# Tracing the stages of an edge step from the oldest quad to the newest

## The chip, the cores and the metric

The kernel runs on one core of a Trainium2 chip. Its time is the device time of one execution in microseconds; a kernel's time is the median of its runs. Before the change it is 5046.02 us (11 runs, 5038.25 to 5059.39). The engines are TensorE (PE in the profile, its weight loads PEld), VectorE (DVE), ScalarE (ACT), GpSimd (POOL) and the DMA queue of SyncE (SP). Each takes its instructions in a fixed order, and an instruction that waits holds those behind it on its engine.

## The reference

Two graph layers over 12,500 nodes of 64 features and 400,000 edges sorted by `dst`. The first is an edge-conditioned message layer with a residual and layer norms, the second two rounds of degree-normalized neighbour sums, a linear layer and another norm:

```python
x_t = _mlp2(x, W1n, b1n, W2n, b2n)
e_t = _mlp2(edge_attr, W1e, b1e, W2e, b2e)      # 32 -> 64 -> 64, leaky_relu 0.1
msgs = x_t[src] * e_t * dp_scale
aggregated = jax.ops.segment_sum(msgs, dst, num_segments=num_nodes)
out = x + aggregated * res_w                    # then layer norm, gamma, beta
...
x = _layernorm(x + out)
...
for _ in range(2):
    msgs = edge_weight[:, None] * h[col]
    h = jax.ops.segment_sum(msgs, row, num_segments=n)
x = _layernorm(x + (h @ W.T + b))
```

`edge_weight` is the product of the inverse square roots of the degrees of the two ends; every node also has a loop to itself.

## The kernel before

**Three phases.** First comes a short one with the node network, whose output goes to a table in DRAM, `xt_tab`. The edge phase follows, to about 4262 us, then the second hop, to the end (5049 us), which is matmuls on TensorE (lines 1221 and 1232) over the adjacency that the edge phase has written to DRAM.

**The edge phase** goes through the edges in "quads" of 12 chunks of 128 edges, 261 quads from the last edge to the first. A quad passes four stages:

- `hidden` (first layer of the edge network): two products on PE into two PSUM banks `pw` (line 624), ACT scales them into `z` (634), DVE takes the maximum (638). `z` has two buffers, the edge features `eat` have three; their load (line 614, SP's queue) is issued two steps ahead and needs the buffer of the quad three before to be free.
- `message`, in two halves: the second layer on PE into a bank `pe` (bias 648, product 650), then DVE multiplies it by the gathered node rows `xg` into `msgs` (659). `xg` has four buffers.
- `level1`: DVE compares the destinations with a range of 32 (one-hot, 674), PE sums the messages per destination into `pl` (684), ACT copies it to `tot` (693).
- `level2`: a second one-hot (DVE, 703) and matmuls that add `tot` into `ring` (713), an accumulator in one PSUM bank.

One step `t` of the loop traces the stages of four different quads: `hidden` of `order[t]`, `message` of the one before, `level1` of the one two before and `level2` of the one three before. Around these five units (two of them are the halves of `message`) it interleaves other work. The step is cut into 15 slots, three to a unit; a unit is traced at the first of its three slots. Each of the first 12 slots traces one gather (line 592): an indirect DMA on POOL of 128 rows of `xt_tab` for the quad two steps ahead. Then the slot traces its share of two generators. `adjacency` builds the dense adjacency by one-hot matmuls (DVE 859 and 910, PE 920, ACT 935, store 944), and `hop1` multiplies finished parts of it (PE 1117, 1129, 1246). After the units come, when the adjacency is done, up to three `scatter_store` preparations for the second hop (DVE 1055, 1059 and 1069, PE 1062 and 1078, ACT 1081), and every ten steps or so the norm of finished nodes (`nodes`, from line 757 on), which reads and clears part of `ring`.

**What sets the order.** The program is traced in this order, and a planner then puts each engine's instructions into their final order by a simulated timeline; units are traced with a priority 500 ahead of the rest. All PSUM users but `ring` share seven banks under one tag.

**The pace of the gathers** is set by hand. `marks` lists the last matmul of each finished message half and of each finished adjacency block, in traced order; when a gather is traced, the one eight before it is made to wait for the mark traced last:

```python
gates.append(got)
if len(gates) > GATE and marks:          # GATE = 8
    tc.add_manual_dep(gates[-GATE - 1], marks[-1].name, ...)
```

`a_target` spreads the adjacency so that it is done about ten steps before the last quad (`LEAD`); after that only messages put down marks.

Of the kernel before, what the change touches and what calls it, by code (L numbers as in the profile page):

```python
# [35 lines left out]
NQ = -(-NCH // QC)  # L36
# [162 lines left out]
def tile_fast(  # L199
# [327 lines left out]
    def bank(shape, name):  # L527

        n = math.prod(shape[1:])
        t = banks.tile([P, 512], F32, name=name, tag="bank")[:, :n]  # L530
        if len(shape) == 3:
            t = t.rearrange("p (a b) -> p a b", b=shape[2])
        elif len(shape) == 4:
            t = t.rearrange("p (a b c) -> p a b c", b=shape[2], c=shape[3])
        return t
# [81 lines left out]
    def hidden(q):  # L617
        def f():
            z = hs[q] = edgep.tile([P, 2, SCC * P], F32, name="z")
            ea_q = eas.pop(q)  # L620
            pws = [bank([P, SCC * P], f"pw{h}") for h in range(2)]
            for h in range(2):
                rows = slice(D * h, D * (h + 1))
                nc.tensor.matmul(  # L624
                    pws[h],
                    w1ab[rows, h, :],
                    ea_q[rows],
                    start=True,
                    stop=True,
                    tile_position=(D * h, 0),  # L630
                )

            for h in range(2):
                nc.scalar.activation(  # L634
                    z[:, h, :], pws[h], AF.Identity, bias=b1s, scale=SLOPE
                )
            for h in range(2):
                nc.vector.scalar_tensor_tensor(  # L638
                    z[:, h, :], pws[h], b1, z[:, h, :], op0=ALU.add, op1=ALU.max
                )  # L640

        return f

    def message(q, h):
        def f():
            z = hs[q]
            pe = bank([P, 2, SCC, D], "pe")
            nc.tensor.matmul(pe, ones_b, b2p, start=True, stop=False)
            for c in range(SCC):
                ended = nc.tensor.matmul(  # L650
                    pe[:, :, c, :],
                    z[:, h, c * P : (c + 1) * P],
                    w2,
                    start=False,
                    stop=(c == SCC - 1),
                )
            marks.append(ended.ins)
            k = 2 * SCC
            nc.vector.tensor_mul(  # L659
                msgs[q % 3][:, k * h : k * (h + 1), :D],  # L660
                pe.rearrange("p s c d -> p (s c) d"),
                xgs[q][:, k * h : k * (h + 1), :],
            )
            if h == 1:
                del hs[q], xgs[q]

        return f

    def level1(q):
        def f():  # L670
            _, rel = seg[q // SEGQ]
            c0 = (q % SEGQ) * QC
            oh = edgep.tile([P, QC, REL], F32, name="oh1")
            nc.vector.tensor_tensor(
                oh,
                iota_f[:, None, :REL].to_broadcast([P, QC, REL]),
                rel[:, c0 : c0 + QC, None].to_broadcast([P, QC, REL]),
                op=ALU.is_equal,
            )
            pl = bank([P, D + 1], "pl")  # L680
            m = msgs[q % 3]
            for s in range(4):
                for c in range(SCC):
                    nc.tensor.matmul(  # L684
                        pl[REL * s : REL * (s + 1), :],
                        oh[:, s * SCC + c, :],
                        m[:, s * SCC + c, :],
                        start=(c == 0),
                        stop=(c == SCC - 1),
                        tile_position=(0, REL * s),  # L690
                    )
            tot = edgep.tile([P, D + 1], F32, name="tot")
            nc.scalar.copy(tot, pl)
            tots[q] = tot

        return f

    def level2(q):
        def f():
            lo, hi = QWIN[q]  # L700
            n = hi - lo + 1
            oh = edgep.tile([P, 4 * P], F32, name="oh2")
            nc.vector.tensor_scalar(
                oh[:, : n * P],
                iota_f[:, : n * P],
                float(P * lo),
                qn[:, q : q + 1],
                op0=ALU.add,
                op1=ALU.is_equal,
            )  # L710
            tot = tots.pop(q)
            for w in range(lo, hi + 1):
                nc.tensor.matmul(
                    ring[:, w % RING, :],
                    oh[:, (w - lo) * P : (w - lo + 1) * P],
                    tot,
                    start=False,
                    stop=False,
                    skip_group_check=True,
                )  # L720

        return f
# [562 lines left out]
    order = list(range(NQ - 1, -1, -1))  # L1285
# [8 lines left out]
    def take(q):  # L1294

        k = q // SEGQ
        if k not in seg:
            load_seg(k)
        load_ea(q)
        return gathers(q)  # L1300
# [30 lines left out]
    for t in range(NQ + 3):  # L1331
        units = []
        if t + PRE < NQ:
            more = take(order[t + PRE])
        else:
            more = iter(())
        if t < NQ:
            units += [hidden(order[t])]
        if 0 <= t - 1 < NQ:
            units += [message(order[t - 1], 0), message(order[t - 1], 1)]  # L1340
        if 0 <= t - 2 < NQ:
            units += [level1(order[t - 2])]
        if 0 <= t - 3 < NQ:
            units += [level2(order[t - 3])]
        if 0 <= t - ZERO < 2 * HT:
            with tc.issue_after(last_load[0]):
                zero_table(t - ZERO)
        lead = 1 + (LEAD - 1) * min(1.0, t / RAMP)
        a_target = a_total * min(1.0, (t + lead) / NQ)
        a_step = max(0.0, a_target - a_spent) / max(1, len(units))  # L1350
        h_step = H_RATE / max(1, len(units))
        a_goal, h_budget = a_spent, 0.0
        parts = -(-QC // len(units))
        a_step, h_step = a_step / parts, h_step / parts
        for u in range(parts * len(units)):
            if u % parts == 0:
                with tc.high_priority(PRIO):
                    units[u // parts]()
            next(more, None)
            a_goal += a_step  # L1360
            while a_live and a_spent < a_goal:
                c = next(a_gen, None)
                if c is None:
                    a_live = False
                else:
                    a_spent += c
            h_budget += h_step
            while h_live and h_budget > 0:
                try:
                    c = next(h_gen)  # L1370
                except StopIteration:
                    h_live = False
                    break
                if c is None:
                    h_budget = 0.0
                    break
                h_budget -= c
        for _ in more:
            pass
        if a_spent >= a_total:  # L1380
            if not spc:
                counts.close()
                scatter_start(
                    main.enter_context(tc.tile_pool(name="spp", bufs=1)), bank
                )
                narrow()
                dpools[0] = ctx.enter_context(tc.tile_pool(name="h2e", bufs=H2E, side="right"))
                early = [load_dense(*d, 0) for d in dense[:H2E]]
            for _ in range(PREPS):
                if prepped < EARLY:  # L1390
                    scatter_store(sparse[prepped])
                    prepped += 1

        q_done = order[t - 3] if t >= 3 else None
        if q_done is not None:
            top = QWIN[q_done - 1][1] if q_done > 0 else -1
            while groups and groups[0][0] > top:
                lo, hi = groups.pop(0)
                with tc.high_priority(PRIO if hi <= 5 else 0):
                    nodes(lo, hi)  # L1400
                ln_done[0] = lo
# [950 lines left out]
```

## Time and profile before

| what | us |
|---|---|
| median of 11 runs | 5046.02 |
| the profiled execution | 5050.39 |
| its span in the profile | 5048.7 |
| first gather starts | 70.2 |
| last gather ends on POOL | 4262.0 |
| second hop's matmuls start | 4322.0 |

Shares of the span: PE 87%, POOL 75%, DVE 65%, ACT 45%; mean granted clock of TensorE 0.911. The second part of the page cuts the span into 40 slices of 126 us; each digit is a busy share in tenths, and the PEclk row is the granted clock in tenths:

```profile
PE   5776889989989898988997999697788978999997
DVE  7887778766658686887777787766777756100004
ACT  3887777545545454654554443333322123100003
POOL 6777767777777777777777777777777765688885
PEclk7888999999999898978997999798898967999998
```

The slices 1 to 34 are the node network and the edge phase, the rest the seam and the second hop. A row read across shows which engine is full where; that an engine is below 9 does not show that it waits, since a gather of 0.94 us with its fixed 0.30 us to the next reads as 7.

### The profile page before, as it was taken

Reading aid. Unit: us, or ns where it says so; the run is one execution under the profiler, and the core shown is the slowest. Engines: PE = TensorE matmul, PEld = TensorE weight load, DVE = VectorE, ACT = ScalarE, POOL = GpSimd, SP = SyncE. Lnnn points to the kernel's source line nnn. Section 1 sums busy time; section 2 is a strip of 40 time slices with the busy share of each in tenths; the row PEclk is TensorE's granted clock in tenths of the full one; section 3 lists DMA queues with packets and bytes.
Section 4 is the critical chain, followed back from the end, with each engine's and each line's share of the span. In section 5 each row is a group of like instructions: output and inputs, shape, how many; then the busy total and the mean of one; then the engine's idle time right before and its main releaser. Section 6 shows DMA issues by size and latency. Waiting matters only on the chain. (4 is left out here: it accounts for less than half of the span.)

```text
span 5048.7 us, 94126 instructions
## 1 busy us (share of the span) xinstructions
PE 4410.5 (87%) x31344; PEld 2581.9 (51%) x31344; DVE 3269.0 (65%) x11086; ACT 2265.0 (45%) x7868; POOL 3793.4 (75%) x3607
## 2 busy tenths in 40 slices
PE   5776889989989898988997999697788978999997
PEld 3443455555546465645554555354455555444443
DVE  7887778766658686887777787766777756100004
ACT  3887777545545454654554443333322123100003
POOL 6777767777777777777777777777777765688885
PEclk7888999999999898978997999798898967999998
DMA  5877788766657576646664554353333253999998
GB/s 140 187 166 135 143 160 158 150 129 147 144 127 152 121 152 130 125 85 150 144 126 103 121 127 101 83 120 88 64 79 75 65 145 99 229 211 213 206 200 222
DMA packets 1254835, 696.95 MB, mean 138 GB/s; under 512 B 593468, under 2 KB 1188144, under 8 KB 1253312
## 3 DMA queue, kind: packets, MB, share of 16 engines
q1 hardware_dynamic: 1104032, 566.91, 46.7%
q0 software_dynamic: 150304, 123.92, 16.1%
q8 instruction: 248, 4.06, 0.3%
q14 instruction: 251, 2.06, 0.2%
HBM read 494.67 MB, written 195.83 MB: 137 GB/s over the span
## 5 line engine op out<-in xcount | busy, mean ns | idle before, releaser
L592 POOL DMA_INDIRECT xg<-xt_tab,si x3125 | 3127.3, 1001 | 1006.1 <-issue 467.2
L935 ACT ACTIVATE stage<-pa 128x391 fp8e4<-128x391 f32 x3077 | 1511.7, 540 | 1132.5 <-PE pa L920 1078.8
L910 DVE TENSOR_SCALAR oh<-iota_b,colT 128x391 bf16<-128x391 bf16 x5556 | 1605.1, 333 | 202.9 <-PE pa L920 199.2
L920 PE MATMUL pa<-oh,koh 128*128 128x391 bf16 (+2 forms) x6054 | 1272.8, 368 | 248.5 <-DVE oh L910 72.5
L920 PEld LDWEIGHTS <-koh 128*128 128x128 bf16 (+2 forms) x6054 | 604.1, 150 | 621.7 <-issue 346.4
L935 ACT ACTIVATION_READ_ACCUMULATOR stage<-pa 128x1 f32 x3077 | 746.8, 247 | 0.0
L1117 PE MATMUL hacc_p<-at,gp 128*128 128x512 fp8e4 (+1 forms) x2425 | 642.8, 393 | 89.2 <-ACT gp L744 45.6
L659 DVE TENSOR_TENSOR msg<-pe,xg 128x384 f32<-128x384 f32 x522 | 289.6, 555 | 545.9 <-DMA xg<-xt_tab,si 342.6
L1492 POOL DMA_INDIRECT hop_tab<-tot,first x317 | 493.4, 1556 | 100.6 <-issue 94.2
L650 PEld LDWEIGHTS pe<-w,z 128*128 128x128 f32 x3132 | 461.4, 208 | 74.7 <-issue 52.0
L650 PE MATMUL pe<-w,z 128*128 128x128 f32 x3132 | 472.9, 291 | 0.0
L1221 PE MATMUL acc<-at,gp 128*128 128x512 fp8e4 (+1 forms) x2000 | 445.9, 376 | 0.0
L1117 PEld LDWEIGHTS <-gp 128*128 128x128 bf16 x2425 | 230.8, 102 | 389.4 <-issue 136.0
L859 DVE TENSOR_TENSOR koh<-iota_k,keyT 128x512 bf16<-128x512 bf16 (+3 forms) x920 | 384.2, 419 | 0.0
L634 ACT ACTIVATE z<-pw,b1s 128x384 f32<-128x384 f32 x522 | 292.2, 616 | 204.2 <-PE pw L624 199.7
L684 PE MATMUL pl<-msg,oh 128*32 128x65 f32 x6264 | 281.0, 229 | 111.9 <-DVE msg L659 108.1
L624 PE MATMUL pw<-eat,w1ab 64*128 64x384 f32 x1044 | 362.7, 600 | 12.1 <-DVE msg L659 7.1
L1129 PE MATMUL hacc_p<-at,gp 128*64 128x512 fp8e4 (+1 forms) x2425 | 365.1, 389 | 0.0
L1600 DVE TENSOR_TENSOR pot<-po,dis 128x256 f32<-128x256 f32 (+2 forms) x26 | 10.5, 408 | 538.4 <-PE po L1594 538.4
L638 DVE SCALAR_TENSOR_TENSOR z<-pw,b,z 128x384 f32<-128x384 f32 x522 | 312.5, 607 | 45.6 <-ACT z L634 45.6
L684 PEld LDWEIGHTS pl<-msg,oh 128*32 128x32 f32 x6264 | 228.5, 112 | 210.1 <-DVE msg L659 95.3
L1221 PEld LDWEIGHTS <-gp 128*128 128x128 bf16 x2000 | 188.3, 99 | 227.3 <-issue 28.8
(218 smaller groups left out, 3954.8 us busy)
## 6 DMA issues: line engine op xcount, KB each, us to landing
adj<-stage SPq DMA_DIRECT2D x390, 391.0 KB
at<-adj SPq DMA_DIRECT2D x97, 896.0 KB
at<-adj SPq DMA_DIRECT2D x168, 512.0 KB
eat<-in_eaq_dram SPq DMA_DIRECT2D x261, 192.0 KB
xg<-xt_tab,si POOLq DMA_INDIRECT x3125
at<-adj SPq DMA_DIRECT2D x96, 256.0 KB
at<-adj SPq DMA_DIRECT2D x24, 832.0 KB
at<-adj SPq DMA_DIRECT2D x24, 768.0 KB
```

What stands on the lines that cost most here:

```text
L592: got = nc.gpsimd.indirect_dma_start(out=xg[:, i, :], out_offset=None, in_=xt_tab, in_offset=bass.IndirectOffsetOnAxis(ap=si[:, c : c + 1] ...
L624: nc.tensor.matmul(pws[h], w1ab[rows, h, :], ea_q[rows], start=True, stop=True, tile_position=(D * h, 0),)
L650: ended = nc.tensor.matmul(pe[:, :, c, :], z[:, h, c * P : (c + 1) * P], w2, start=False, stop=(c == SCC - 1),)
L684: nc.tensor.matmul(pl[REL * s : REL * (s + 1), :], oh[:, s * SCC + c, :], m[:, s * SCC + c, :], start=(c == 0), stop=(c == SCC - 1), tile_ ...
L859: nc.vector.tensor_tensor(t[:, :, :n], iota_8[:, :, :n] if w == 8 else iota_k[:, : w * FA, :n], keyT[:, None, j0 : j0 + n].to_broadcast([P ...
L910: nc.vector.tensor_scalar(oh, iota_b, colT[:, i % P : i % P + 1], None, op0=ALU.is_equal)
L920: ended = nc.tensor.matmul(to, key, oh, start=(j == 0), stop=(j == caps[g] - 1), tile_position=(0, r0),)
L935: nc.scalar.activation(stage[:, u, :], pa, AF.Identity, saturate=True, accum_out=sums[:, u : u + 1],)
L1117: nc.tensor.matmul(acc[:, :w], gp[:kk, lo + i, 0:2, :].rearrange("p t d -> p (t d)"), t[:kk, i, :w], start=start, stop=False, skip_group_c ...
L1129: nc.tensor.matmul(acc[D * h : D * (h + 1), :w], gp[:kk, lo + i, 2, :], t[:kk, i, :w], start=False, stop=False, skip_group_check=True, til ...
L1221: nc.tensor.matmul(acc[:, :w], gp[:kk, wi, 0:2, :].rearrange("p t d -> p (t d)"), t[:kk, wi - lo, :w], start=first and n == 0, stop=False, ...
L1492: nc.gpsimd.indirect_dma_start(out=hop_tab[(q * QC + i) % HT], out_offset=bass.IndirectOffsetOnAxis(ap=first[:, q - Q0, i : i + 1], axis=0 ...
```

## The change

Only the order in which a step traces its five units is turned round: level 2 of the oldest of the four quads first, then level 1, the two message halves, and the newest quad's first layer last. Which quads a step works on is as before, as are the gathers, the two generators between the units, the gate and the work after the units.

```diff
@@ -1334,14 +1334,14 @@
             more = take(order[t + PRE])
         else:
             more = iter(())
+        if 0 <= t - 3 < NQ:
+            units += [level2(order[t - 3])]
+        if 0 <= t - 2 < NQ:
+            units += [level1(order[t - 2])]
+        if 0 <= t - 1 < NQ:
+            units += [message(order[t - 1], 0), message(order[t - 1], 1)]
         if t < NQ:
             units += [hidden(order[t])]
-        if 0 <= t - 1 < NQ:
-            units += [message(order[t - 1], 0), message(order[t - 1], 1)]
-        if 0 <= t - 2 < NQ:
-            units += [level1(order[t - 2])]
-        if 0 <= t - 3 < NQ:
-            units += [level2(order[t - 3])]
         if 0 <= t - ZERO < 2 * HT:
             with tc.issue_after(last_load[0]):
                 zero_table(t - ZERO)
```

## The prediction

> **What bounds the kernel now.** I read the page's engine shares first, then its costliest groups, then POOL's waits stretch by stretch, then the busy time by stretch, and last the chain of work around the end of the edge phase. The first lines are from the page and from the view of one source line (L592, the gather of 128 node rows); the columns are busy time, mean ns | idle before, releaser, and below them min/median/max ns.
>
> ```profile
> PE 4410.5 (87%) x31344; PEld 2581.9 (51%) x31344; DVE 3269.0 (65%) x11086; ACT 2265.0 (45%) x7868; POOL 3793.4 (75%) x3607
> L592 POOL DMA_INDIRECT xg<-xt_tab,si x3125 | 3127.3, 1001 | 1006.1 <-issue 467.2
> L592 POOL DMA_INDIRECT xg<-xt_tab,si x3125: 938/944/3579, 70.2 to 4261.1; - x196
> ```
>
> PE has the largest share, but POOL issues gathers one behind the other from 70 us to 4262 us: 3127 busy + 1006 idle = 4133 of 4192 us. Most of that idle time is a fixed 0.30 us ahead of each gather (3125 x 0.30 = 938). So a gather costs 1.30 us and a quad of twelve 15.6 us, and only about 1006 - 938 = 68 us are real waiting. Where it is shows in POOL's waits (total, times, longest) in 500 to 820, 820 to 4040 and 4040 to 4265 us:
>
> ```profile
> POOL xg L592 <- PE pa L920: 41.0, 76, 6.8
> ...
> POOL xg L592 <- PE pa L920: 142.9, 469, 0.3
> ...
> POOL xg L592 <- PE pe L650: 33.8, 9, 9.5
> ```
>
> In the 3200 us in the middle no gather waited beyond its 0.3 us. Beyond 0.3 us each, the early stretch holds 41.0 - 76 x 0.3 = 18.2 us (waiting for adjacency blocks), the late one 33.8 - 9 x 0.3 = 31.1 us (waiting for the messages' matmuls). Busy time by stretch (PE, PEld, DVE, ACT, POOL, granted clock, DMA share, GB/s):
>
> ```profile
> 820.00:2000.00 1180.00, 1103.94 (x8103) 651.27 (x8101) 840.86 (x2856) 630.25 (x2251) 902.06 (x913) 0.95 0.66 140
> 2000.00:4040.00 2040.00, 1760.34 (x12431) 1078.27 (x12429) 1536.44 (x5394) 864.29 (x2868) 1563.31 (x1565) 0.90 0.48 104
> 4040.00:4262.00 222.00, 185.15 (x1257) 127.97 (x1255) 123.21 (x246) 65.86 (x121) 148.28 (x141) 0.66 0.45 126
> 4322.00:5049.00 727.00, 698.16 (x5128) 334.21 (x5126) 79.39 (x148) 75.24 (x202) 568.82 (x380) 0.98 0.92 210
> ```
>
> PE is 94% busy up to 2000 us, 86% up to 4040, and the second hop after 4322 is PE's alone. The chain of waits at the seam:
>
> ```profile
> 4261.10 3.18 DMA xg<-xt_tab,si
> ...
> 4264.40 0.57 DVE msg L659
> ...
> 4310.81 4.82 DMA gw_tab<-gwp
> ...
> 4322.02 3.56 PE acc L1221 x16
> ```
>
> The last gather lands, the last message is multiplied, and 58 us later the second hop starts. So the time is: end of the gathers (4262.0) + tail (60.0) + second hop (726.7) = 5048.7 us, and 1.7 us around the span make the profiled 5050.4. This execution lies 4.4 us above the median of the runs, 5046.0; I make the sum against 5050.4 and subtract 4.4.
>
> **The change part by part.** No instruction is added or removed. Per quad the moved stages issue: hidden 4 PE passes (two fp32 products), 2 ACT, 2 DVE; the two messages 14 PE passes and 2 DVE; level 1 24 PE passes, 1 DVE, 1 ACT; level 2 some 4 PE passes and 1 DVE. None issues a DMA. A step has 15 slots, with adjacency blocks and first-hop batches between the stages. Hidden moves from slot 0 to 12, the messages from 3 and 6 to 6 and 9, level 1 from 9 to 3, level 2 from 12 to 0. The planner may re-sort, but PE holds nearly to the traced order: in one step (time, duration)
>
> ```profile
> 2002.49 0.33 PE L648 MATMUL pe<-b2p,ones_b 128*128 128x384 bf16 x1
> ...
> 2006.85 0.96 PE L684 MATMUL pl<-msg,oh 128*32 128x65 f32 x24
> ...
> 2008.61 0.92 PE L624 MATMUL pw<-eat,w1ab 64*128 64x384 f32 x4
> ...
> 2015.26 0.33 PE L648 MATMUL pe<-b2p,ones_b 128*128 128x384 bf16 x1
> ```
>
> messages, level 1, next hidden, next messages follow as traced.
>
> 1. Distances between stages of one quad. Hidden to message and message to level 1 shrink from 18 slots to 9, level 1 to level 2 from 18 to 12. Taken quad by quad from the timeline (quads 60 to 240), the first-layer matmul starts a median 21.2 us ahead of its message matmul; 9/18 of it is 10.6 us. What must fit is pw start to the end of the second DVE pass over z: median 4 to 6 us. Message done to level 1 is 12.5 us at the 5th percentile in quads 20 to 120; 10.6 us less still leaves 2. In the later quads PE reaches level 1 when its message is just done (median 1 to 4 us), so level 1 would now hold PE; behind it queue adjacency blocks, whose marks POOL waits for. But that lock is to the gathers themselves. I replayed the loop's arithmetic to find the block or message each gather waits for: margins are at least 0.3 us from 560 to 820 us, 7 to 1200, 11 to 2000 and mostly over 20 afterwards. Cost 0. Without that cover it is 4 us a quad over 140 quads, 560 us; I leave that end out, since a PE that falls behind finds its messages ready and stops no more.
>
> 2. Messages three slots later. Where compute rides behind the gathers (the message waits 342.6 us in all for xg), DVE's in-order stop at the message comes 3/15 of a 15.4 us step later, so compute stands 3.1 us further when adjacency ends near 4040 us. Bounds 0 to -3.1; I take -2. The gather buffer (four quads) is freed 3.1 us later; the gather that reuses it starts 19.4 us or more after that now. Cost 0, the 19.4 us hide it.
>
> 3. The late gate. A gather waits for the last mark traced when the eighth after it is traced. After the adjacency that is a message: gather 7 of quad k+2 waited for message k; now gather 10 does. The last stall ended at 4225.47; 29 gathers remained, taking 36.6 us (1.26 each). Three more ahead of the gate are -3.8 us, against which level 2 and level 1 (0.4 + 1.0 us) and three slots of hop work (0.9) now precede the message in the step instead of hidden (1.65): +0.7. But the last quad's message matmul ends at 4260.1, against 4264.3 for the gather's landing, and without background work the shorter distance (z 4.3 us, level 2 and 1 fill 1.4) stops PE 1 to 2 us in each of the last two steps. Bounds +1 to -4; I take -2, between.
>
> 4. The eat load of quad q+3 on SP waits for hidden q, 12 slots (12 us) later; behind it on SP queue adjacency stores and loads. Loads stand a median 43.5 us ahead of use (36.5 at the 5th percentile); 24 remain. Cost 0; were it late, PE would stop at pw.
>
> 5. DVE work that stretches gathers. The mean gather is 57 ns above its median, 178 us in all, and DVE's lines move against them. Matched one by one in the timeline, gathers that overlap level 1's one-hot (0.55 us on DVE) run 139 ns over 945, those that overlap a message 24 ns. Number and length of these instructions stay: 0, with +-0.14 us x 261 = 36 us as far ends if all or none of the one-hots collided.
>
> The Trainium skill, SBUF — State Buffer, section "SBUF: two separate sides", speaks against moving DVE work here: a two-port DVE operation locks GpSimd out for its whole length, so POOL's descriptors wait. By that rule, if both one-hots (0.55 + 0.35 us) fell from the gaps onto gathers, it would be up to 235 us; the trace's 139 ns is far below, and the total does not use the rule.
>
> Sum: 0 - 2 - 2 + 0 + 0 = -4: 5050.4 - 4 = 5046.4, on the scale of the runs **5042 us**.
>
> **Rivals.** Faster: the early stall goes too. For: POOL's 18.2 us there are waits for PE, and level 1 and 2 first hand back buffers sooner. Against: the gates on adjacency blocks are the same, and PE's work is unchanged. 5042 - 18 = 5024; with the late 31 us too, 4997 at most, which PE's 37 us of idle time in 4040 to 4262 hardly allows.
>
> Slower: PE stops for z where it has nothing to spare, 100 to 2000 us. Quad by quad, pw to z exceeds 9 us by 27 us in all over quads 5 to 120, and 7 us by 36 (single quads take 16 and 22 us). If the distance shrinks to 7, 36 us of PE idle come before margins of 0.3 us (560 to 820) and 7 us (to 1200): 5046 + 36 - 7 = 5075. It decides once PE loses over 7 us there. For: 94% busy, and one list of waits already has a 14.7 us stop for z. Against: the medians fit.
>
> No change: the planner restores the old order: 5046. Against it stands PE's order above.
>
> **How the numbers follow.** Forecast 0.38 (own range 5034 to 5054), no change 0.04, faster rival 0.27, slower rival 0.31. A measurement of this kernel can tell about 0.2%, 10 us, from no change. Both signs beside it hold over half, so the range is 5012 to 5085: the faster case down past 5024, the slower one past 5075 by 10 us, about what one quad of 16 or 22 us adds. Same: 0.36 + 0.04 = 0.40; 0.01 of the forecast falls off at each end, so faster 0.28, slower 0.32.
>
> **What would show it.** Right: gathers still back to back from 820 to 4040 us at 1.30 us each; PE's order per step ring, pl, pe, pw; the late waits of POOL under 31 us; the last gather's end at 4255 to 4262. Point 1 is wrong if POOL waits for pa between 820 and 4040; the slower rival shows as PE waiting for z (L638) before pe. A gather mean off 1001 ns by over 5 ns (16 us) would overturn point 5 and the forecast with it.

## The result, and the profile after

| | us | against before |
|---|---|---|
| kernel before, median of 31 runs | 5047.47 | |
| changed kernel, median of 8 runs | 5120.41 | 1.0146 (95%: 1.0135 to 1.0157) |
| its profiled execution | 5111.43 | span 5109.7, before 5048.7 |

The change makes the kernel 1.5% slower, 73 us, where 4 us less were forecast; the forecast's range ended at 5085 us. The two profiled executions differ by 61 us. The page and the gathers' line of the changed kernel, in the columns of the first lines shown before:

```profile
PE 4487.8 (88%) x31344; PEld 2615.9 (51%) x31344; DVE 3292.0 (64%) x11086; ACT 2267.7 (44%) x7868; POOL 3775.2 (74%) x3607
L592 POOL DMA_INDIRECT xg<-xt_tab,si x3125 | 3109.9, 995 | 1063.2 <-issue 495.4
L592 POOL DMA_INDIRECT xg<-xt_tab,si x3125: 938/944/3580, 71.5 to 4301.0; - x196
```

Same number of instructions everywhere, gathers a little shorter (995 for 1001 ns), and yet the last one ends 40 us later (4301.9 for 4262.0) and PE is busy 77 us longer. POOL's waits (total, times, longest) in 500 to 820, 820 to 4040 and 4040 to 4305 us:

```profile
POOL xg L592 <- PE pa L920: 38.2, 83, 4.6
...
POOL xg L592 <- PE pe L650: 6.7, 10, 1.3
...
POOL xg L592 <- PE pa L920: 151.6, 479, 3.4
...
POOL xg L592 <- PE pe L650: 75.0, 11, 16.0
```

Beyond 0.3 us each, the middle stretch holds 151.6 - 479 x 0.3 = 7.9 us: the gathers still run back to back there. The late one holds 75.0 - 11 x 0.3 = 71.7 us, where it was 31.1. Busy time by stretch (PE, PEld, DVE, ACT, POOL, granted clock, DMA share, GB/s):

```profile
2000.00:4040.00 2040.00, 1765.77 (x12434) 1083.23 (x12433) 1549.87 (x5400) 863.20 (x2872) 1561.19 (x1572) 0.91 0.49 104
4040.00:4302.00 262.00, 225.76 (x1162) 141.26 (x1162) 117.30 (x233) 64.12 (x115) 140.24 (x138) 0.54 0.38 106
4382.00:5110.00 728.00, 698.37 (x5126) 334.23 (x5124) 77.54 (x148) 75.37 (x201) 567.48 (x380) 0.98 0.91 210
```

From 2000 to 4040 us and in the second hop next to nothing has changed. Between them lie 60 us more: 40 up to the last gather, with the granted clock at 0.54 where it was 0.66, and 20 behind it (80 us from there to the second hop, where it was 60). The chain of waits at the seam:

```profile
4296.38 1.57 PE pw L624 x2
4297.95 0.79 PE pl L684 x6
...
4323.40 0.63 PE pl L684 x19
...
4370.36 5.31 DMA gw_tab<-gwp
...
4381.87 3.56 PE acc L1221 x16
```

Before, the chain came out of the last gather's landing; now it comes out of PE, which is 22 us behind the last gather. From message to message, quads 253 to 256 took 19.7, 18.4, 18.2 and 18.9 us before and take 22.8, 25.8, 25.7 and 24.2 now; from message 249 (4082.4 and 4082.9 us) to message 260 it is 182.6 us before, 240.8 now. That is 58 of the 61 us.

One late step on PE shows why. A "pass" is one matmul record; a float32 product has two. Before (start, us, line, out<-in, count):

```profile
4184.78 1.65 PE L624 MATMUL pw<-eat,w1ab 64*128 64x384 f32 x4
...
4186.66 1.35 PE L650 MATMUL pe<-w,z 128*128 128x128 f32 x6
...
4188.71 0.83 PE L650 MATMUL pe<-w,z 128*128 128x128 f32 x6
4189.47 0.73 PE L684 MATMUL pl<-msg,oh 128*32 128x65 f32 x18
```

Each unit stands as a block (the view ends inside level 1's 24 passes). The changed kernel:

```profile
4212.61 0.64 PE L684 MATMUL pl<-msg,oh 128*32 128x65 f32 x4
4213.18 0.50 PE L648 MATMUL pe<-b2p,ones_b 128*128 128x384 bf16 x1
4213.62 0.42 PE L684 MATMUL pl<-msg,oh 128*32 128x65 f32 x2
4213.97 0.80 PE L650 MATMUL pe<-w,z 128*128 128x128 f32 x2
4214.70 0.43 PE L684 MATMUL pl<-msg,oh 128*32 128x65 f32 x2
4215.05 0.80 PE L650 MATMUL pe<-w,z 128*128 128x128 f32 x2
...
4219.52 1.64 PE L624 MATMUL pw<-eat,w1ab 64*128 64x384 f32 x2
```

The planner has taken level 1's 24 passes apart and put them in pairs between those of the messages and the first layer. Two of them take 0.42 us; a block of 24 took 0.96 us at 2006.85 before. PE hardly stands still here (in four late steps it is idle for 6.3 of 99.9 us), it is slow. This mixing of the units' passes is called weaving below, and an unbroken row of one unit's passes a piece. In PE's order, from the first product of `scatter_store` on, level 1 lies in 23 pieces before and in 89 now (of 13 quads); up to there it lies in 300 and 343 (of 248 quads), so that it is hardly woven before the late steps.

### The profile page after: what moved, and what is told of

The parts are those of the page before. It is cut to its first block, busy times and chain, and to the rows that moved or that the text cites. A ratio compares the mean times of both kernels' runs of the same rounds, so it can differ in the third digit from the quotient of the medians.

```text
span 5109.7 us, 94092 instructions
## 1 busy us (share of the span) xinstructions
PE 4487.8 (88%) x31344; PEld 2615.9 (51%) x31344; DVE 3292.0 (64%) x11086; ACT 2267.7 (44%) x7868; POOL 3775.2 (74%) x3607
## 4 chain that ended last, share of the span: by engine, by line
PE 44%; DMA 8%; DVE 5%; POOL 2%; issue 2%; ACT 1%; DVEq 0%; SPq 0%; POOLq 0%; ACTq 0%
PE acc L1221 8%; PE pa L920 7%; DMA xg<-xt_tab,si 7%; PE hacc_p L1117 5%; PE acc L1232 4%; PE pe L650 4%; PE pl L684 3%; PE hacc_p L1129 3%; PE pw L624 2%; PE pc L1246 2%; POOL xg L592 2%; DVE oh L910 2%; PE pk L1078 1%; PE pe L648 1%; PE ring L713 1%
## 5 line engine op out<-in xcount | busy, mean ns | idle before, releaser
L935 ACT ACTIVATION_READ_ACCUMULATOR stage<-pa 128x1 f32 x3077 | 761.2, 259 | 0.0
L650 PE MATMUL pe<-w,z 128*128 128x128 f32 x3132 | 501.1, 297 | 0.0
L684 PE MATMUL pl<-msg,oh 128*32 128x65 f32 x6264 | 339.7, 242 | 92.8 <-DVE msg L659 83.0
L684 PEld LDWEIGHTS pl<-msg,oh 128*32 128x32 f32 x6264 | 259.3, 120 | 241.1 <-issue 107.8
L1129 PE MATMUL hacc_p<-at,gp 128*64 128x512 fp8e4 (+1 forms) x2425 | 382.4, 386 | 0.0
```

Source lines behind the costliest of these rows:

```text
L650: ended = nc.tensor.matmul(pe[:, :, c, :], z[:, h, c * P : (c + 1) * P], w2, start=False, stop=(c == SCC - 1),)
L684: nc.tensor.matmul(pl[REL * s : REL * (s + 1), :], oh[:, s * SCC + c, :], m[:, s * SCC + c, :], start=(c == 0), stop=(c == SCC - 1), tile_ ...
L935: nc.scalar.activation(stage[:, u, :], pa, AF.Identity, saturate=True, accum_out=sums[:, u : u + 1],)
L1129: nc.tensor.matmul(acc[D * h : D * (h + 1), :w], gp[:kk, lo + i, 2, :], t[:kk, i, :w], start=False, stop=False, skip_group_check=True, til ...
```

## The experiments

**The first runs, with the device in another condition.** Theory W says that the weaving of level 1 costs the time, rival O the order as such, rival M a loss in the main stretch. The kernels, each an edit of the changed one:

```diff
 e1, e2: only one part of the steps in the new order
+        if t < 249:            # e2: t >= 249
             (new order)
+        else:
+            (old order)
 e3: PE's products of a unit wait in the planned order for the unit before
     (last_unit[0] is the last product traced of that unit)
-                with tc.high_priority(PRIO):
+                with tc.high_priority(PRIO), ExitStack() as chain:
+                    if t >= 249 and u:
+                        chain.enter_context(tc.issue_after(last_unit[0]))
                     units[u // parts]()
 e4: hidden, level2, level1, message, message
 e6: level2, message, message, level1, hidden
```

> The new order of the stages up to step 248, the old one from step 249 on (the late stage, where the adjacency is done and each step prepares three quads for the second hop). Theory W (PE's instructions of the late stage are put in an order that alternates level 1's matmuls with the message's, and that costs 5 to 8 us a step): the loss is gone, 5040 to 5052 us, POOL's waits in 4040 to 4265 us under 35 us. Rival O (the turned order as such is slower in the late stage, because the first layer comes last and level 1 first): the same 5040 to 5052. Rival M (the loss is made before 4040 us, where the edge phase does its adjacency): 5110 to 5125.

> The old order up to step 248, the new one from step 249 on. W and O: the whole loss, 5112 to 5128 us, with the granted clock at 0.5 through most of 4150 to 4320 us. M: 5040 to 5052.

> The new order throughout; from step 249 on, each unit's PE instructions are queued behind the last PE instruction of the unit traced before it, so level 1's twelve matmuls, the two message halves and the first layer each stand together, in the new order. W: the loss is nearly gone, 5043 to 5060 us, late steps of 18 to 20 us. O: 5105 to 5125, late steps still 24 us and more. M: 5105 to 5125.

> The first layer first again, as before the change; then level 2, level 1, the messages. In the planned order of the late stage level 1's matmuls stand in 51 pieces, against 89 in the changed kernel and 23 before. W: part of the loss by the number of pieces, 28/66 of 73 us, so 5070 to 5090 us. O, if it is the first layer's place that costs: 5040 to 5055; if it is level 1's place ahead of the messages: 5105 to 5125. M: 5105 to 5125, or 5047 if it is the first layer's place.

In these runs the kernel before took 6575.77 us in place of 5047, and the ratios to it were 0.9423 (0.9396 to 0.9451) for e1, 0.9986 for e2, 0.9331 for e3 and 0.9315 for e4. None of the theories had said that. The next three sets of runs, with e1 and e3 again, with e6 and with the changed kernel itself, met the same condition:

> New order of the stages in the steps before 249, old order from 249 on. Ratios to the kernel before of the same call, since the first call's device ran that kernel at 6576 us. Theory W (the loss arises only in the steps from 249 on, where level 1's products are woven between others): 0.998 to 1.001. Rival M (the loss is made before, in the main stretch): 1.012 to 1.016. If the device is again one at 6.5 ms: 0.94, as before, and nothing is told of the late steps.

> The changed kernel, with TensorE's products of each unit from step 249 on held behind the last product of the unit traced before it, so that the traced order stays and the weaving goes. Theory W: ratio 0.998 to 1.003; level 1's 24 products of a quad run within 1 to 1.6 us in the late steps, and a late step takes 18 to 21 us where the changed kernel's took 24 to 31. Rival O (what costs is the order as such, the first layer's products last in the step, woven or not): 1.011 to 1.016, late steps of 24 us and more.

> Order level 2, both messages, level 1, first layer: the first layer still comes last, but in the planned order of TensorE level 1's products lie in 28 pieces instead of 89 (before: 23). Theory W: ratio 0.997 to 1.004. Rival O (the first layer at the end of the step costs): 1.010 to 1.016. A third, L (level 1 ahead of the messages delays them, whatever the weaving): also 0.997 to 1.004, told from W by e3b, which has level 1 ahead of the messages and for which L says 1.008 or more.

> The changed kernel itself, as an anchor: on the device of the first measurement it took 1.0146 of the kernel before. If the devices of the two calls before (6570 us for the kernel before) still run so, the sum from their own runs is: message 249 at 5110 us (mean of the two runs with the new order up to there), 274.6 us to message 260 (the run with the new order from 249 on) and 786.5 us behind it, 6171 us, ratio 0.939. On a device like the first: 1.013 to 1.016.

> The changed kernel with TensorE's products of each unit from step 249 on held behind the last product of the unit traced before it. Expected by the device that the run lands on. On one like the first (5046 us for the kernel before), theory W (weaving costs): ratio 0.996 to 1.003, rival O (the order as such costs): 1.011 to 1.016. On one like the last three calls' (6459 to 6576 us): 0.932 to 0.940, a repetition that tells nothing new.

Before took 6570.51, 6458.63 and 6570.93 us; e1b 0.9418, e3b 0.934, e6 0.9845, the changed kernel 0.9461 (0.9434 to 0.9489), e3c 0.9346. There the change is a gain of 5%, and what makes it one is that level 1 stands ahead of the messages (e4, with the first layer first but level 1 ahead of the messages, gains 6.9%; e6, with level 1 behind them, 1.5%). These ratios answer another question and aren't set beside the result; what they show of the hardware stands at the end. One thing carried over: from message 249 to message 260 the woven order took 274.6 us (e2 and the changed kernel alike), the same order unwoven 223 to 225 us (e3, e3b, e3c). But the old order took 275 to 277 us there (e1b, e1), so in this condition the stretch doesn't show what the change costs.

**The decisive runs** found a device like that of the result (before: 5047.57 us).

```diff
 e7: level 1 in the late steps in another form, woven as before
+            for i in range(QC if late else 0):      # late: t >= 249
+                u = REL * min(i, QC - 4)
+                nc.tensor.matmul(
+                    pl, ohf[:, u : u + P], m[:, i, :], start=(i == 0), stop=(i == QC - 1)
+                )
+            for s in range(0 if late else 4):       # the narrow products
 e8: as e3, in all steps
-                    if t >= 249 and u:
+                    if u:
```

> The changed kernel again, as the anchor of this call: ratio to the kernel before 0.94 to 0.95 on a device like those of the last four calls; 274 us from message 249 to message 260, level 1's products of a late quad spread over 12 us.

> The changed kernel with the traced order of TensorE's products kept from step 249 on. Theory W (weaving costs): 225 us from message 249 to message 260 as in the three earlier runs, and the time 35 to 60 us below the changed kernel's of this call. Rival O (the order costs, woven or not): within 15 us of the changed kernel.

> From step 249 on level 1's 24 products write all 128 rows from 128 columns instead of 32-column tiles (they add mixed one-hots, so the sums of those quads are left wrong); the planned order stays woven, 88 pieces for the changed kernel's 89. Theory S (what weaving costs is the change of form: beside a 32-column product a 128-column one takes 0.51 us instead of 0.21 and the 32-column one 0.25 instead of 0.03 to 0.11): some 8 pieces a step by 0.30 us and 8 by 0.14, 3 to 4 us less in each of 8 steps, so 240 to 252 us from message 249 to 260. Rival D (the message is late because other products lie between its own, whatever their form): 268 to 275 us.

> The traced order of TensorE's products kept in every step, not only from 249 on. Theory W alone: like e3d, within 15 us, since only 331 pieces of level 1 in 249 quads lie before step 249 (1.3 to a quad) and the gathers set the pace there. Rival: a fixed order makes TensorE wait for messages in the main stretch, 30 us or more slower than e3d.

| run | us | ratio (95%) | message 249 to 260, us |
|---|---|---|---|
| changed kernel (a1b) | 5123.04 | 1.0154 (1.0137 to 1.0171) | 242.3 |
| e3d, late steps unwoven | 5054.92 | 1.0018 (1.0007 to 1.0030) | 181.6 |
| e7, woven, no narrow products | 5091.29 | 1.0094 (1.0057 to 1.0130) | 226.2 |
| e8, unwoven everywhere | 5058.33 | 1.0031 (1.0017 to 1.0044) | 180.4 |

The stretches named in the expectations (274, 225 and 240 to 275 us) came from the other condition and don't apply here; only the differences are compared. e3d takes 68 us off the changed kernel, with the order as traced and level 1 in one piece a quad: W stands, O falls. e8 lies 3.4 us from e3d, within its 15; its rival falls too. A late step of e3d on PE:

```profile
4207.51 1.53 PE L684 MATMUL pl<-msg,oh 128*32 128x65 f32 x24
4208.97 0.50 PE L648 MATMUL pe<-b2p,ones_b 128*128 128x384 bf16 x1
4209.26 1.49 PE L650 MATMUL pe<-w,z 128*128 128x128 f32 x6
4210.54 0.53 PE L648 MATMUL pe<-b2p,ones_b 128*128 128x384 bf16 x1
4210.86 1.15 PE L650 MATMUL pe<-w,z 128*128 128x128 f32 x6
4211.94 0.92 PE L624 MATMUL pw<-eat,w1ab 64*128 64x384 f32 x4
```

The same 24 + 14 + 4 passes that spread over 12 us there take 5.4 us here, from 4207.51 to 4212.86. The next lines hold the whole of PE over four late steps (message 253 to 257) in before, the changed kernel, e3d and e7; the columns are the window and its length, PE's busy time, then those of PEld, DVE, ACT, POOL, and the granted clock:

```profile
4172.66:4246.33 73.67, 65.18 (x441) 45.27 (x440) 44.77 (x87) 26.35 (x47) 52.66 (x51) 0.65 0.40 112
```

```profile
4196.69:4296.62 99.93, 93.58 (x465) 57.60 (x465) 46.96 (x89) 27.01 (x48) 56.03 (x55) 0.50 0.31 86
```

```profile
4175.67:4252.57 76.90, 66.09 (x464) 48.09 (x464) 46.85 (x89) 26.34 (x48) 55.17 (x51) 0.64 0.38 110
```

```profile
4183.77:4276.31 92.54, 83.41 (x465) 63.12 (x464) 46.60 (x89) 27.01 (x48) 55.18 (x53) 0.60 0.32 92
```

A late step follows what PE does in it: PE is busy for 16.3 of 18.4 us before, 23.4 of 25.0 in the changed kernel, 16.5 of 19.2 in e3d, 20.9 of 23.1 in e7 (each a quarter of its window). DVE, ACT and POOL are busy for nearly the same time in all four. And the three units hold all of PE's 7.1 us more: the same windows for `pl`, `pe` and `pw` alone, before,

```profile
4172.66:4246.33 73.67, 3.33 (x76) 2.67 (x76) 0.65 (x3) 0.65 0.40 112
...
4172.66:4246.33 73.67, 12.48 (x56) 10.51 (x48) 4.44 (x9) 0.65 0.40 112
...
4172.66:4246.33 73.67, 6.90 (x17) 2.32 (x18) 4.57 (x8) 4.21 (x8) 0.65 0.40 112
```

and in the changed kernel:

```profile
4196.69:4296.62 99.93, 17.93 (x96) 9.15 (x96) 0.86 (x4) 0.50 0.31 86
...
4196.69:4296.62 99.93, 21.64 (x56) 12.55 (x48) 4.47 (x8) 0.50 0.31 86
...
4196.69:4296.62 99.93, 13.15 (x17) 3.99 (x17) 4.87 (x9) 4.65 (x8) 0.50 0.31 86
```

The first number after the length is PE's: 3.33 + 12.48 + 6.90 = 22.7 us becomes 52.7, 7.5 us more in each of the four steps (20 of level 1's 96 passes fall outside the window of before, about 0.2 us a step). Level 1 alone takes over four times as long, the messages 1.7 and the first layer 1.9 times.

What a piece costs shows in the times from the end of one PE pass to the end of the next in the late steps, at half the clock: a message pass behind a message pass ends 0.21 us after it, behind a level-1 pass 0.51 us. A level-1 pass ends 0.25 us after a message pass, but 0.11 us (median) after another of its kind. So one insertion costs about 0.30 + 0.14 = 0.44 us. With 89 - 23 = 66 pieces more that is an estimated 29 us, half of the 58. This fits the Trainium skill, TensorEngine Tiling (Array Packing), section "Key Properties", by which a change of the tiling mode drains TensorE; the page gives no price, the trace does: 0.44 us for there and back.

Most of the rest is speed that a unit has only as a block. At the same half clock the first layer's four passes take 1.65 us together before (at 4184.78), and two of them alone 1.64 us in the changed kernel (at 4219.52): in the block passes end in twos, 0.01 us apart, and in a woven pair 0.64 us apart. Level 1's 24 passes take 1.53 us as a block at half the clock (e3d, at 4207.51), and every woven pair 0.42 us.

How much of it is the clock can be estimated. Summed from pass end to pass end over the four steps, the three units take 5.5 us a step before and 11.8 us in the changed kernel. In whole blocks at half the clock throughout they would take 6.35 us (level 1 1.46, the messages' biases 0.75 and products 2.56, the first layer 1.58, from the blocks of before and e3d that ran at half the clock). So about 0.8 us of the 6.2 a step is the lower clock, and 5.4 us come of the weaving itself.

e7 tests the change of form, since its level-1 passes no longer use the narrow one (two lines of a woven step at half the clock):

```profile
4198.10 0.52 PE L685 MATMUL pl<-msg,oh 128*128 128x65 f32 x2
4198.42 0.74 PE L650 MATMUL pe<-w,z 128*128 128x128 f32 x2
```

An exchange (two passes of level 1 and two of a message) takes 0.85 us from end to end in e7, in place of 1.08 us. That is four times the 0.21 us of an unbroken row in e7, so in one form the alternation itself costs nothing: S holds for the exchange. But the edit has a price of its own: a level-1 pass of the wide form ends 0.21 us after another of its kind, where the narrow one takes 0.11 us in pairs and 0.06 in a block. That is at least 24 x 0.1 = 2.4 us a step. So the 16 us that e7 takes off the stretch (242.3 to 226.2; by the changed kernel's other profile, 240.8, it is 14.6), where S had said 22 to 35 and D nothing, are what is left of the gain behind that price, and they don't tell how large S's part is. The first layer's products, in a form of 64 rows, remain woven in e7.

The clock falls as well. The changed kernel's stays at one half for 167 us, e3d's comes back to full in every late step. The changed kernel over these 167 us:

```profile
4152.80:4320.00 167.20, 158.05 (x761) 97.20 (x760) 73.07 (x138) 41.16 (x74) 77.57 (x76) 0.50 0.28 77
```

Here PE is busy for 158.05 of 167.20 us at a granted clock of 0.50, and for the last 35 us of them no gap of its records is over 0.02 us. At half the clock six passes of a message take 1.49 us in place of 0.83, and the first layer's four 1.65 in place of 0.92. The Trainium skill, TensorE: Matmul & The Clock Gate, section "What's actually happening", has the full clock return after about 3.4 us of sustained busy time; by busy time alone it would have been back within the first few of these 167 us. The measurement decides: a PE that is busy by these records did not bring the clock back. Why it stays low under woven passes was not tested.

**Where it arises, and an order that isn't woven.** The last runs, with before at 5042.72 us:

> New order up to step 248, old order from 249 on. On a device like the first (the kernel before at 5046 us): theory W 0.998 to 1.003 (nothing is lost before step 249, and nothing that lasts is gained), rival M (a loss before) 1.010 and more. On one like those of the earlier calls: 0.94 as before.

> Old order up to step 248, new order from 249 on. On a device like the first: theory W 1.012 to 1.017, the whole loss of the change from its last 15 steps alone; rival M below 1.005. On one like those of the earlier calls: 0.999 as before.

> Level 2, messages, level 1, first layer: nothing is held, but the planned order has level 1 in 28 pieces from step 249 on. On a device like the first: by the rule read from the last call (a late step is as long as TensorE's products in it, 5.6 us of a step's own at 23 pieces, 12.7 at 89, so 0.11 us for each piece of the eleven steps) 28 pieces give 0.5 us a step, 5 us in all: ratio 0.999 to 1.004. Rival O' (the first layer last in the step delays it): 1.010 and more.

| run | us | ratio (95%) | message 249 to 260, us |
|---|---|---|---|
| e1c, new then old | 5060.33 | 1.0029 (1.0016 to 1.0042) | 179.6 |
| e2b, old then new | 5102.23 | 1.0116 (1.0099 to 1.0133) | 240.7 |
| e6b, level 2, messages, level 1, first layer | 5047.35 | 1.0006 (0.9996 to 1.0015) | 189.0 |

The two parts add up to the whole, 0.29% + 1.16% = 1.45%: four fifths come from the last 15 steps, one fifth from before them, where W had said nothing (e1c lies inside W's 0.998 to 1.003 all the same; e2b lies just under its 1.012). e6b keeps the first layer last and level 2 first, is held by nothing, and costs nothing that can be told from before: only where level 1 stands ahead of the messages does the planner take it apart (89 pieces in the changed kernel and 51 in e4, but 28 in e6b and 23 before). Its late stretch is 6.4 us longer than before's, where 5 were expected.

The small part lies in quads 35 to 47, 670 to 900 us, where PE is at its fullest. In 600 to 1000 us the gathers' waits beyond 0.3 us sum to 17.8 us before, 17.9 in e2b and 14.7 in e6b, but 25.9 and 33.7 in the changed kernel's two profiles, 34.5 in e1c, 34.0 in e3d, 34.4 in e8 and 42.3 in e7. All of these have level 1 ahead of the messages. That an unwoven order (e8) has it too says that it is another thing than the late loss. A message that comes later in its step, where no gather had time to spare, would do it, and in e6b, which doesn't have it, the messages keep their old slots; but level 1 keeps its slots there as well, so this cause is argued, not shown. The lists of waits name the message's matmul more often: before

```profile
POOL xg L592 <- PE pe L650: 1.5, 5, 0.3
```

and in e1c

```profile
POOL xg L592 <- PE pe L650: 9.0, 13, 1.3
```

Beyond 0.3 us each that is 5.1 us in e1c; the waits for adjacency blocks grow too, from 17.8 to 24.2 us. Why was not followed. No kernel here beats the one before on a device of this kind.

## Why the prediction was wrong

**The step that failed** is the reading that carries the part on the change: "The planner may re-sort, but PE holds nearly to the traced order", shown by one step at 2002 us, and with it the price in point 3, where level 2 and level 1 were put ahead of the message as blocks of 0.4 + 1.0 us against a first layer of 1.65. At 2002 us adjacency blocks lie between the units, and the order holds. From step 249 on these blocks are gone, and the planner weaves level 1, the messages and the first layer. That it does so because they are ready together and of the same priority is read from the program; the runs show that the loss is gone where the order is held (e3d). The steps of 4040 us and later, the ones that mattered, were never looked at for their order. In place of 1.4 us a step for level 1 and 2 against 1.65 there came 7.5 us a step of longer products; point 3's -2, bounded at +1, was +58. Its signs fell with it: the late waits of POOL are 71.7 us where under 31 were to show it right, and the last gather ends at 4301.9 us, not by 4262.

**Point 1** (shorter distances, cost 0) was right from 900 to 4040 us and wrong before: of its margins, the 0.3 us given for 560 to 820 us was none. It cost about 15 us by e1c (0.0029 x 5043), 8 to 17 by POOL's waits in all but e7 (24.5). What the point had feared, PE held by level 1, isn't what these runs show: from 600 to 1000 us no product of level 1 waits for its message in the changed kernel, e1c, e3d or e8. Its own sign shows all the same: from 820 to 4040 us POOL's waits for adjacency blocks hold 7.9 us beyond 0.3 us each, before 142.9 - 469 x 0.3 = 2.2. By what the margin is used up stays open.

**Point 2** (3 us further ahead at 4040): the last gather of quad 248 came 3.5 us earlier in the changed kernel's profile, but 0.2 us earlier in a1b, and 2.2 and 7.5 us later in e3d and e1c. In e2b, with the old order up to there, it came 8.2 us earlier, so single profiles scatter by more than the 3 us; the gain isn't shown.

**Point 4** held: no product of the first layer waits for its `eat` load in either list. **Point 5**: gathers in 2000 to 4040 us took a mean of 999.3 ns in both runs with the old order there, 991.9 to 996.1 in six with the new one, some 5 to 12 us gained over 1560 gathers. It is small against the loss. The named limit, a mean off 1001 ns by more than 5 ns, was crossed on the side of a gain (995 ns in the changed kernel).

**The rivals.** The slower one, 5075, put its stall in 100 to 2000 us at PE's wait for `z`. A stall came in that stretch, of about half its 29 us, but the `z` waits didn't grow: PE's waits of `pe` for `z` go from 8.3 us to none in 100 to 2000 us. The faster one and "no change" fell. (The faster one's 4997 us is counted from 5046, its 5024 from 5042; nothing rests on the difference.) That the range ended at 5085 came of taking the late steps as locked to the gathers: once PE's own work in a step grows past the gathers' time, nothing in the sum bounds the loss but the number of late steps. The trace of before could have shown it: PE is busy for 65 of 74 us in four late steps, 88%, so that whatever lengthens its passes lengthens the step.

## What to carry to other kernels

Where a planner sorts what was traced, a change of the traced order must be priced from the planned order, and in each stage apart: units that other work keeps in blocks in one stage can be taken apart in the next. Here matmuls of one tile form were fastest in one block: each level-1 piece put between 128-column products cost 0.44 us at half the clock, in a stage where PE had 2 us in 18 to spare, and products that run fast side by side in a block lost that as well. A hold on the order (e3d) kept the block whole, and an order with the narrow products behind the messages (e6b) nearly so.

## What was not expected of the hardware

The same program takes 5.04 or 6.57 ms, and not by the chip alone: on the chip with number 6 the kernel before took 6459 us in one set of runs and 5043 us in a later one. In the longer condition its mean granted clock is 0.80 where it is 0.91 otherwise, and a record of PE can be as short as ever while what waits for it comes late. In e2 (first runs) level 1 and the copy that waits for it:

```profile
2139.55 0.96 PE L684 MATMUL pl<-msg,oh 128*32 128x65 f32 x24
...
2148.09 0.69 PE L713 MATMUL ring<-tot,oh 128*128 128x65 f32 x2 [6.60 <-ACT tot L693]
...
2147.82 0.21 ACT L693 COPY tot<-pl 128x65 f32<-128x65 f32 x1 [5.30 <-remote]
```

The products' records end at 2140.5, the copy starts at 2147.8. From the end of level 1's products to the copy it is a median 0.04 us in before and in e2b, and 5.19 us in e2, 4.84 in e6, both with level 1 behind the messages; with it ahead of them, 1.65 to 2.42. The order with the shorter delay is the one that wins 5% in this condition; that the delay is what makes the difference is likely but not shown, and why it arises the runs don't tell. A verdict on an order of matmuls is one for the condition that it was measured in, and the time of the kernel before, taken beside it, says which that is.
